# Local attention in a decoder kernel: softmax weights turned by VectorE in squares of 32, value products over 32 keys with the values stationary

## The chip, the cores and the metric

The kernel runs on one core of one Trainium2 chip. The metric is the device time of one execution in microseconds; the time before is 2144.68 us, the median of three runs (2144.33 to 2145.66). The engines of the core are TensorE (PE; the profile lists its weight loads apart, as PEld), VectorE (DVE), ScalarE (ACT), GpSimd (POOL) and SyncE (SP, which here only issues DMAs).

## The reference, cut to what matters

A decoder works on x of shape (8, 256, 128) in float32: a state-space layer, a cross attention, and then, in six layers, a local attention and a feed-forward block, each added to x. Only the local attention is touched. Per layer and batch it has 16 heads of 64 numbers and windows of 32 tokens; a window's 32 queries see its own 32 keys and the 32 of the window before:

```
q, k = l2norm(q) * q_scale, l2norm(k) * k_scale    # then rotary turns and scales
bk2, bv2 = look(bk), look(bv)                      # window before + own window: 64 keys
sim = einsum('bhwie,bhwje->bhwij', bq, bk2) * 8
sim = where(mask, -max, sim)
attn = softmax(sim, -1)
out = einsum('bhwij,bhwje->bhwie', attn, bv2)      # this product is what the change recasts
x = out.reshape(b, n, 1024) @ Wo + x
```

## The kernel before, in words

Stages 1 and 2 (state space, cross attention) fill the first 530 us or so and are not touched. Stage 3 holds the six layers. It is a pipeline over 48 "runs", one for each layer and batch. The order of the work in a run is written out by hand in the list `slots` (L1338 to L1359): four quarters, each with a query or key projection, a transposition, a piece of attention for one of four tiles, and a piece of the feed-forward block of an earlier pair of batches (`"ff"`). PE and DVE take their instructions in exactly that order (`manual_schedule`, L1482); ACT and POOL are ordered by the framework's planner; SP issues the DMAs.

Names on the way of the change, for one run n:

- `query_key` (L1041): two projections of 512 columns into PSUM (`qk_ps`, L1035), then DVE multiplies by the rotary tables (L1052, L1053), POOL adds the halves (L1056), ACT squares (`sq`, L1058), which on ACT comes after DVE's two reads of the same PSUM tile. `normalise` (L1084, POOL) and `turn` (8 transpositions on PE into `qkT_ps`, L1091, copied out by ACT) follow. `value` (L1076) projects the values of 128 tokens and ACT copies them to `v`.
- `scores` (L1126), per half `wh` of 128 tokens: 64 small products, each of 64 rows by 32 stationary columns with 64 moving ones, in eight tiles of the array (two row groups `e` by four column groups `i`). They fill the two-bank PSUM tile `s3_ps`. That tile and `o3_ps` come from `ps_two` (L72), of which there is one buffer only, so whoever fills it waits until the one before has been read out.
- Per tile t = (wh, g), g a group of eight heads: `masked` (L1147, DVE adds the mask into `pw`), `peak` (DVE maximum, POOL subtracts, L1161), `weigh` (ACT exponential), `add_weights` (DVE sum and reciprocal, POOL multiplies, L1174).
- `turn_weights` (L1176): four 128x128 transpositions on PE (L1181) and one ACT copy (L1185) put the 64 keys on the partitions.
- `place` and `spread` (L1103): per tile nine DMAs of `v` into `vz` (L1120), so that each window's 64 keys lie on 64 partitions once for each head parity; six fixed buffers are zeroed in `begin` (L1407).
- `attend` (L1188), per half: 64 products (L1198) with the weights stationary (64 rows by 32 columns) and the values moving (64 columns), in the same eight tiles. The outputs come out with queries on partitions; two DVE transpositions in squares of 32 (L1206) turn them into `oT`.
- `project_out` (L1208): eight products with `Wo` (L1212) and the addition to x. Since a square of 32 turns only inside itself, `load` (L987) brings `Wo` in eight DMAs with its rows permuted.

A matmul of float32 stands in the profile as two LDWEIGHTS and MATMUL pairs, a transposition as one; 64 products of `attend` are 128 pairs.

Of the kernel before, what the change touches and what calls it, by code (L numbers as in the profile page):

```python
# [9 lines left out]
FP = mybir.dt.float32  # L10
# [4 lines left out]
P = 128  # L15
# [35 lines left out]
def decoder_kernel(ctx: ExitStack, tc: tile.TileContext, a: dict, out: bass.AP):  # L51
# [934 lines left out]

    def load(d):  # L987
        wo = pools3["w"].tile([P, NHB, D], FP, name="wo3")

        for i in range(4):  # L990
            for g in range(2):
                f = (4 * g + i) * P
                nc.sync.dma_start(
                    out=wo[32 * i : 32 * i + 32, 4 * g : 4 * g + 4, :],
                    in_=a["L0_ffn_Wo"][d][f : f + P].rearrange("(k r) e -> r k e", r=32),
                )
        w1 = pools3["w"].tile([P, 2 * DFF], FP, name="w1")
        nc.sync.dma_start(out=w1, in_=a["L0_ffn_W1"][d])
        w2 = pools3["w"].tile([P, 3, D], FP, name="w2")
        nc.sync.dma_start(  # L1000
            out=w2[:, 0:2, :], in_=a["L0_ffn_W2"][d][0:256].rearrange("(k p) e -> p k e", p=P)
        )
        nc.sync.dma_start(out=w2[: DFF - 256, 2, :], in_=a["L0_ffn_W2"][d][256:DFF])
        wts[d] = wo, w1, w2
# [95 lines left out]
        else:  # L1100
            copied.append(A.copy(fixed3["kz"][:, :, W + tb * P : W + (tb + 1) * P], t3))  # L1101

    def spread(v, wh, g):  # L1103


        vz = fixed3["vzs"].pop(0)
        fixed3["vzs"].append(vz)
        for j in range(4):
            w = 4 * wh + j
            for e in range(2):  # L1110

                at = max(0, (w - 1) * W)
                end = (w + 1) * W
                while at < end:
                    tb = at // P
                    n = min(end, (tb + 1) * P) - at
                    k = e * HD + at - (w - 1) * W
                    src = v[tb][at - tb * P : at - tb * P + n, :]
                    src = src.rearrange("p (k e d) -> p k e d", e=2, d=HD)
                    nc.sync.dma_start(  # L1120
                        out=vz[k : k + n, j, :, :], in_=src[:, 4 * g : 4 * g + 4, e, :]
                    )
                    at += n
        return vz

    def scores(n, wh):  # L1126

# [18 lines left out]

    def masked(n, t):  # L1147
        wh, g = tiles3[t]
        shape = [P, 4, 2, 2 * W]
        pw = pools3["b"].tile(shape, FP, name="pw", bufs=5)  # L1150
        V.tensor_tensor(
            pw,
            got[n]["s_ps"][:, :, g * 256 : (g + 1) * 256].rearrange("p e (w k) -> p w e k", w=4),
            fixed3["mask"][:, 4 * wh : 4 * wh + 4, :].unsqueeze(2).to_broadcast(shape), ALU.add,
        )
        got[n]["pw", t] = pw, pools3["b"].tile([P, 2, 4, 2], FP, name="mx", bufs=5)

    def peak(n, t):
        pw, mx = got[n]["pw", t]
        V.tensor_reduce(mx[:, 0], pw, AX.X, ALU.max)  # L1160
        G.tensor_tensor(pw, pw, mx[:, 0].unsqueeze(3).to_broadcast([P, 4, 2, 2 * W]), ALU.subtract)  # L1161

    def place(n, t):
        got[n]["vz", t] = spread([got[n].get(("v", tb)) for tb in range(2)], *tiles3[t])

    def weigh(n, t):
        pw, mx = got[n]["pw", t]
# [2 lines left out]
    def add_weights(n, t):  # L1170
        pw, mx = got[n]["pw", t]
        V.tensor_reduce(mx[:, 1], pw, AX.X, ALU.add)
        V.reciprocal(mx[:, 1], mx[:, 1])
        G.tensor_tensor(pw, pw, mx[:, 1].unsqueeze(3).to_broadcast([P, 4, 2, 2 * W]), ALU.mult)  # L1174

    def turn_weights(n, t):  # L1176

        pw, mx = got[n]["pw", t]
        t_ps = ps_s("pT_ps")
        for j in range(4):  # L1180
            T.transpose(  # L1181
                t_ps[:, j * P : (j + 1) * P], pw[:, j].rearrange("p e k -> p (e k)"), ident
            )
        pT = pools3["b"].tile([P, 4, P], FP, name="pT", bufs=4)
        turned.append(A.copy(pT.rearrange("p j q -> p (j q)"), t_ps))  # L1185
        got[n]["pT", t] = pT

    def attend(n, wh):  # L1188

        o_ps = ps_two("o3_ps")  # L1190
        for g in range(2):
            pT, vz = got[n]["pT", 2 * wh + g], got[n]["vz", 2 * wh + g]
            for j in range(4):
                for i in range(4):
                    for e in range(2):
                        r = slice(e * HD, (e + 1) * HD)
                        c = (4 * g + j) * HD
                        T.matmul(  # L1198
                            o_ps[i * W : (i + 1) * W, e, c : c + HD],
                            lhsT=pT[r, j, i * W : (i + 1) * W], rhs=vz[r, j, i, :],  # L1200
                            start=True, stop=True, tile_position=(e * HD, i * W),
                        )

        oT = got[n]["oT", wh] = pools3["b"].tile([P, 2, 2, 4 * HD], FP, name="oT3")
        for g in range(2):
            V.transpose(oT[:, g], o_ps[:, :, g * 256 : (g + 1) * 256])  # L1206

    def project_out(n, wh):  # L1208
        d, b = seq[n]
        y_ps = ps_s("y3_ps")  # L1210
        for hb in range(NHB):
            T.matmul(  # L1212
                y_ps[:, :P], lhsT=wts[d][0][:, hb, :],
                rhs=got[n]["oT", wh][:, hb // 4, (hb // 2) % 2, :].rearrange(
                    "p (w h q) -> p h w q", w=4, h=2
                )[:, hb % 2],
                start=(hb == 0), stop=(hb == NHB - 1),
            )
        half = slice(wh * P, (wh + 1) * P)
        V.tensor_tensor(  # L1220
            batch(x3, b)[:, half], batch(x2 if d == 0 else x3, b)[:, half], y_ps[:, :P],
            ALU.add,
        )
        if wh:
            got[n].clear()
# [88 lines left out]
    def finish(p, b=None):  # L1314
# [22 lines left out]
    q, k = 0, 1  # L1337
    slots = [  # L1338

        (weigh, 0, 1), (place, 0, 1), (value, 1, 0), (scores, 0, 1),  # L1340
        ("end", 0), (masked, 0, 2), (masked, 0, 3), (squares, 1, k, 0), (turn, 1, q, 0),
        (peak, 0, 2), ("end", 1), ("ff",), (turn_weights, 0, 0), (add_weights, 0, 1),
        (query_key, 1, k, 1), (root, 1, k, 0), (normalise, 1, k, 0),

        ("end", 1), (weigh, 0, 2), (place, 0, 2), (project_out, -1, 0),
        (attend, -1, 1), (squares, 1, k, 1), (turn, 1, k, 0),
        (peak, 0, 3), ("end", 0), ("ff",), (turn_weights, 0, 1), (add_weights, 0, 2),
        (query_key, 2, q, 0), (root, 1, k, 1), (normalise, 1, k, 1), (shift, 3),

        (weigh, 0, 3), (place, 0, 3), (value, 1, 1), (scores, 1, 0),  # L1350
        ("end", 0), (masked, 1, 0), (masked, 1, 1), (squares, 2, q, 0), (turn, 1, q, 1),
        (peak, 1, 0), ("end", 1), ("ff",), (turn_weights, 0, 2), (add_weights, 0, 3),
        (root, 2, q, 0), ("late",), (query_key, 2, q, 1), (normalise, 2, q, 0),

        (weigh, 1, 0), (place, 1, 0), (project_out, -1, 1),
        (attend, 0, 0), (squares, 2, q, 1), (turn, 1, k, 1),
        (peak, 1, 1), ("end", 0), ("end", 1), ("ff",), (turn_weights, 0, 3), (add_weights, 1, 0),
        (query_key, 2, k, 0), (root, 2, q, 1), (normalise, 2, q, 1),
    ]  # L1359
# [36 lines left out]
    def begin():  # L1396

        for name in ("w", "a"):
            pools3[name] = ctx.enter_context(
                tc.tile_pool(name=f"s3{name}", bufs=2, side="right", reuse_waits="tile")  # L1400
            )
        fixed3["kz"] = pools3["a"].tile([P, NHB, W + S], FP, name="kz", bufs=1)
        fixed3["vzs"] = [
            pools3["a"].tile([P, 4, 4, HD], FP, name=f"vz{i}", bufs=1) for i in range(6)
        ]
        for t in [fixed3["kz"]] + fixed3["vzs"]:
            G.memset(t, 0.0)  # L1407
        fixed3["rot"] = pools3["w"].tile([P, 4, 2, HD], FP, name="rot", bufs=1)
        nc.sync.dma_start(out=fixed3["rot"], in_=a["c_rot"])
        for c in range(3):  # L1410
            load_third(0, c)
        load_table3(0)
        load(0)
        yield
        steps = [(shift, 0)]
        for c in range(2):
            for tb in range(2):
                steps += [
                    (f, 0, c, tb) for f in (query_key, squares, root, normalise)
                ]  # L1420
        for f, *args in steps:
            f(*args)
            done.add((f, *args))
            yield
# [48 lines left out]
    with ExitStack() as st:  # L1473
# [8 lines left out]
        with tc.manual_schedule(engines={mybir.EngineType.PE, mybir.EngineType.DVE}):  # L1482
            shift(1)
            for n in range(-1, len(seq)):
                run(n)
            project_out(len(seq) - 1, 0)
            attend(len(seq) - 1, 1)
            for _ in ff:
                pass
            next(end)  # L1490
            project_out(len(seq) - 1, 1)
            tail = feed_forward(DEPTH - 1, NPAIR - 1, 1)
            queue.append(finish(NPAIR - 2))
            while queue:
                next(tail, None)
                next(end)
            for _ in tail:
                pass
            for _ in finish(NPAIR - 1, 1):
                pass  # L1500
# [86 lines left out]
```

## Time and profile before

| what | value |
|---|---|
| median of three runs | 2144.68 us |
| the profiled execution | 2138.47 us |
| its span | 2136.7 us |
| granted TensorE clock, mean | 0.985 |
| stage 3, one run | about 31.3 us (two runs 62.6 us) |

The page gives the busy time of each engine, the chain of work that ended last, and groups of instructions as "line engine operation, out<-in, shapes, count | busy us, mean ns of one | idle time before them and what ended it". "Busy" of PE is no measure of load by itself, since matmuls overlap: a single matmul lasts some 216 ns here from its start to its modelled end, while the next can start a few ns later. Better is the time from the start of one group of matmuls to the start of the next, which the timeline and the chain give.

### The profile page before, as it was taken

The numbers are of one execution on the slowest core, as the hardware profiler recorded it, in microseconds if no ns is written. First come the engines' busy times: TensorE is split into PE (matmuls) and PEld (weight loads), VectorE is DVE, ScalarE is ACT, GpSimd is POOL, SyncE is SP. The second block draws the span as 40 slices with busy tenths as digits, with TensorE's granted clock in tenths as the row PEclk, the third lists the DMA queues.
The fourth block names the chain that finished last, engine by engine and source line by source line (L and its number), as shares of the span: only waits on it lengthen the run. The fifth ranks groups of instructions, "written<-read, shape, count | busy, mean of one in ns | idle before, by whom it ended". The sixth has DMA issues, their size and how long they took to land.

```text
span 2136.7 us, 77541 instructions
## 1 busy us (share of the span) xinstructions
PE 2015.2 (94%) x32582; PEld 1324.2 (62%) x32582; DVE 1728.0 (81%) x2663; ACT 1478.7 (69%) x2654; POOL 1664.9 (78%) x1466
## 2 busy tenths in 40 slices
PE   5899899899989999999999999999999999999986
PEld 3355454455566766667676666767666667676663
DVE  6778888786688888888888888888888888888752
ACT  5767867666667677777677777766777766767654
POOL 4778878887699888888888888888888887888740
PEclk8999999999999999999999999999999999999998
DMA  5433333333244343444434444443444434333330
GB/s 131 90 62 74 68 71 74 70 74 80 55 75 71 68 97 68 78 72 74 89 68 79 70 82 76 75 77 64 94 69 73 76 69 84 64 65 68 61 56 10
DMA packets 455194, 156.11 MB, mean 73 GB/s; under 512 B 402046, under 2 KB 451068, under 8 KB 454716
## 3 DMA queue, kind: packets, MB, share of 16 engines
q1 hardware_dynamic: 454364, 150.76, 37.4%
q8 instruction: 256, 4.19, 0.9%
q14 instruction: 94, 0.77, 0.1%
q10 hardware_dynamic: 480, 0.38, 0.1%
HBM read 55.33 MB, written 1.31 MB: 27 GB/s over the span
## 4 chain that ended last, share of the span: by engine, by line
PE 78%; ACT 10%; DVE 9%; issue 1%; POOL 1%; DMA 0%; ACTq 0%; POOLq 0%; DVEq 0%
PE qk_ps L1035 13%; PE y_ps L1212 8%; PE qkT_ps L1091 8%; PE o_ps L1198 7%; PE f_ps L1282 6%; PE v_ps L1035 6%; PE s_ps L1139 5%; PE pT_ps L1181 3%; PE y L645 3%; PE f_ps L1310 3%; PE o_ps L340 2%; PE s_ps L318 2%; PE k_ps L273 1%; DVE rb L1053 1%; DVE m L625 1%
## 5 line engine op out<-in xcount | busy, mean ns | idle before, releaser
L1056 POOL TENSOR_TENSOR qk<-qk,rb 128x512 f32<-128x512 f32 x384 | 481.3, 1276 | 51.2 <-DVE rb L1053 33.5
L1084 POOL TENSOR_TENSOR qk<-qk,rn 128x1024 f32<-128x1024 f32 x192 | 365.8, 1905 | 11.6 <-ACT rn L99 11.6
L1035 PE MATMUL qk_ps<-wqkv,xs 128*128 128x512 f32 x768 | 363.0, 595 | 1.6 <-ACT kz L1101 1.6
L1161 POOL TENSOR_TENSOR pw<-pw,mx 128x512 f32<-128x512 f32 x192 | 202.1, 1053 | 165.8 <-DVE mx L1160 165.6
L1058 ACT ACTIVATE sq<-qk_ps 128x1024 f32<-128x1024 f32 x192 | 197.1, 1026 | 167.6 <-PE o_ps L1198 114.9
L1052 DVE TENSOR_TENSOR qk<-qk_ps,tab 128x1024 f32<-128x1024 f32 x192 | 229.0, 1193 | 72.5 <-PE qk_ps L1035 71.0
L1053 DVE TENSOR_TENSOR rb<-qk_ps,tab 128x1024 f32<-128x1024 f32 x192 | 233.3, 1215 | 0.0
L1065 DVE TENSOR_REDUCE ss<-sq 128x16 f32<-128x1024 f32 x192 | 229.3, 1194 | 4.8 <-ACT sq L1058 4.8
L1174 POOL TENSOR_TENSOR pw<-pw,mx 128x512 f32<-128x512 f32 x192 | 200.7, 1046 | 39.5 <-ACT fxn L1269 32.0
L1212 PEld LDWEIGHTS y_ps<-oT,wo 128*128 128x128 f32 x1536 | 186.6, 192 | 46.6 <-issue 33.5
L1091 PE MATMUL qkT_ps<-ident,qk 128*128 128x128 f32 x1536 | 210.0, 279 | 3.5 <-POOL qk L1084 3.0
L607 POOL TENSOR_TENSOR dw<-wz 128x512 f32<-128x512 f32 x128 | 133.2, 1041 | 102.8 <-DVE wz L605 98.9
L1206 DVE STREAM_TRANSPOSE oT<-o_ps 128x512 f32<-128x512 f32 x192 | 126.2, 696 | 80.4 <-PE o_ps L1198 80.4
L1035 PEld LDWEIGHTS qk_ps<-wqkv,xs 128*128 128x128 f32 x768 | 131.3, 191 | 96.2 <-issue 93.2
L1212 PE MATMUL y_ps<-oT,wo 128*128 128x128 f32 x1536 | 187.7, 275 | 1.9 <-ACT pT L1185 1.6
L1139 PEld LDWEIGHTS s_ps<-kz,qT 64*32 64x32 f32 x12288 | 137.6, 105 | 76.4 <-issue 36.2
L1035 PE MATMUL v_ps<-wqkv,xs 128*128 128x512 f32 x384 | 180.8, 593 | 0.1
L1091 PEld LDWEIGHTS qkT_ps<-ident,qk 128*128 128x128 f32 x1536 | 165.2, 141 | 23.3 <-POOL qk L1084 3.8
L627 POOL TENSOR_TENSOR mc<-m,rows 128x512 f32<-128x512 f32 x128 | 163.0, 1273 | 13.3 <-PE y L645 5.2
L625 DVE TENSOR_TENSOR_SCAN m<-dw,ab 128x256 f32<-128x256 f32 x256 | 160.6, 669 | 11.9 <-ACT ab L99 8.0
L1198 PE MATMUL o_ps<-vz,pT 64*32 64x64 f32 x12288 | 167.4, 225 | 1.2 <-issue 1.2
L99 ACT ACTIVATE pw<-pw 128x512 f32<-128x512 f32 x192 | 120.7, 629 | 66.9 <-POOL pw L1161 66.9
(209 smaller groups left out, 4082.6 us busy)
## 6 DMA issues: line engine op xcount, KB each, us to landing
vz<-v SPq DMA_DIRECT2D x1152, 64.0 KB, 2.2
rows<-bc_dram SPq DMA_DIRECT2D x128, 256.0 KB, 4.7
vz<-v SPq DMA_DIRECT2D x576, 32.0 KB, 2.3
wqkv<-in_L_ffn_Wqkv SPq DMA_DIRECT2D x18, 512.0 KB, 5.0
wo<-in_L_ffn_Wo SPq DMA_DIRECT2D x48, 64.0 KB, 3.0
w<-in_L_ffn_W SPq DMA_DIRECT2D x6, 341.0 KB, 3.5
t_in<-in_x SPq DMA_DIRECT2D x4, 256.0 KB
wkv<-in_L_xattn_Wkv SPq DMA_DIRECT2D x1, 1024.0 KB
```

What stands on the lines that cost most here:

```text
L1035: T.matmul(pr[:, i * 512 : (i + 1) * 512], lhsT=got[n]["xs"][:, tb * P : (tb + 1) * P], rhs=thirds[seq[n][0], c][:, i * 512 : (i + 1) * 51 ...
L1052: V.tensor_tensor(t, p3, cs, ALU.mult)
L1053: V.tensor_tensor(rb, p3, sn, ALU.mult)
L1056: G.tensor_tensor(t[:, :, o], t[:, :, o], rb[:, :, f], ALU.add)
L1065: V.tensor_reduce(got[n]["ss"][:, 2 * c + tb, :], got[n]["sq"], AX.X, ALU.add)
L1084: G.tensor_tensor(t, t, r, ALU.mult)
L1091: T.transpose(t_ps[:, hb * P : (hb + 1) * P], t[:, 2 * hb : 2 * hb + 2, :].rearrange("p h d -> p (h d)"), ident,)
L1139: T.matmul(s_ps[i * W : (i + 1) * W, e, c : c + 2 * W], lhsT=qT[r, 4 * g + i, j * W : (j + 1) * W], rhs=kz[r, 4 * g + i, k0 : k0 + 2 * W], ...
L1161: G.tensor_tensor(pw, pw, mx[:, 0].unsqueeze(3).to_broadcast([P, 4, 2, 2 * W]), ALU.subtract)
L1174: G.tensor_tensor(pw, pw, mx[:, 1].unsqueeze(3).to_broadcast([P, 4, 2, 2 * W]), ALU.mult)
L1198: T.matmul(o_ps[i * W : (i + 1) * W, e, c : c + HD], lhsT=pT[r, j, i * W : (i + 1) * W], rhs=vz[r, j, i, :], start=True, stop=True, tile_p ...
L1212: T.matmul(y_ps[:, :P], lhsT=wts[d][0][:, hb, :], rhs=got[n]["oT", wh][:, hb // 4, (hb // 2) % 2, :].rearrange("p (w h q) -> p h w q", w=4 ...
```

## The change

`turn_weights` becomes one DVE transposition in squares of 32, from SBUF to SBUF. Inside each square 32 queries by 32 keys change places, so that the keys of a window lie on 32 partitions `i` (a pair of heads) and their two query windows (own and next) lie side by side. `attend` takes the values as the stationary operand (32 rows of keys by 64 columns of one head) and the weights as the moving one (64 columns, or 32 at the edge of a half), and adds up in PSUM over the windows. It is called twice for each half (`part`), each time with two of the four row groups, because each row group writes to its own bank. The outputs come out turned, so an ACT copy takes the place of the DVE transpositions. `pw` changes the order of its axes; `place` fills one `vz` tile per 128 tokens by 16 DMAs; `Wo` is loaded in one DMA; the zeroing goes.

```diff
     def load(d):
-        for i in range(4):
-            for g in range(2):
-                f = (4 * g + i) * P
-                nc.sync.dma_start(out=wo[32 * i : 32 * i + 32, 4 * g : 4 * g + 4, :], ...)
+        nc.sync.dma_start(out=wo, in_=a["L0_ffn_Wo"][d].rearrange("(k p) e -> p k e", p=P))
...
+    def place(n, tb):
+        vz = got[n]["vz", tb] = pools3["a"].tile([P, 4, 2, P], FP, name="vz", bufs=6)
+        src = got[n]["v", tb].rearrange("p (g i c) -> p g i c", g=2, i=4)
+        for w in range(4):
+            for i in range(4):
+                nc.sync.dma_start(
+                    out=vz[i * W : (i + 1) * W, w], in_=src[w * W : (w + 1) * W, :, i, :]
+                )
...
     def turn_weights(n, t):
         pw, mx = got[n]["pw", t]
-        t_ps = ps_s("pT_ps")
-        for j in range(4):
-            T.transpose(
-                t_ps[:, j * P : (j + 1) * P], pw[:, j].rearrange("p e k -> p (e k)"), ident
-            )
-        pT = pools3["b"].tile([P, 4, P], FP, name="pT", bufs=4)
-        turned.append(A.copy(pT.rearrange("p j q -> p (j q)"), t_ps))
+        pT = got[n]["pT", t] = pools3["b"].tile([P, 2, 2 * P], FP, name="pT", bufs=4)
+        V.transpose(
+            pT.rearrange("p e c -> p (e c)"), pw.rearrange("p e w k -> p (e w k)")
+        )
-    def attend(n, wh):
-        o_ps = ps_two("o3_ps")
-        for g in range(2):
-            for j in range(4):
-                for i in range(4):
-                    for e in range(2):
-                        r = slice(e * HD, (e + 1) * HD)
-                        c = (4 * g + j) * HD
-                        T.matmul(
-                            o_ps[i * W : (i + 1) * W, e, c : c + HD],
-                            lhsT=pT[r, j, i * W : (i + 1) * W], rhs=vz[r, j, i, :],
-                            start=True, stop=True, tile_position=(e * HD, i * W),
-                        )
-        oT = got[n]["oT", wh] = pools3["b"].tile([P, 2, 2, 4 * HD], FP, name="oT3")
-        for g in range(2):
-            V.transpose(oT[:, g], o_ps[:, :, g * 256 : (g + 1) * 256])
+    def attend(n, wh, part):
+        o_ps, first = ps_two("o3_ps"), True
+        for js in ((0, 2), (-1, 1, 3) if wh else (1, 3)):
+            for g, j in ((g, j) for g in range(2) for j in js):
+                pT, w = got[n]["pT", 2 * wh + g], 4 * wh + j
+                vz = got[n]["vz", w // 4]
+                lo, hi = max(j, 0) * W, min(j + 2, 4) * W
+                at = max(2 * j + 1, 0) * W
+                for b in range(2):
+                    i = 2 * part + b
+                    r = slice(i * W, (i + 1) * W)
+                    c = g * P
+                    for e in range(2):
+                        T.matmul(
+                            o_ps[e * HD : (e + 1) * HD, b, c + lo : c + hi],
+                            lhsT=vz[r, w % 4, g, e * HD : (e + 1) * HD],
+                            rhs=pT[r, e, at : at + hi - lo],
+                            start=first, stop=bool(g and j == 3), tile_position=(i * W, e * HD),
+                        )
+                first = False
+        if not part:
+            got[n]["oT", wh] = pools3["b"].tile([P, 2, 2, 2 * P], FP, name="oT3")
+        turned.append(A.copy(got[n]["oT", wh][:, part], o_ps[:, :, : 2 * P]))
...
     slots: second quarter
-        ("end", 1), (weigh, 0, 2), (place, 0, 2), (project_out, -1, 0),
-        (attend, -1, 1), (squares, 1, k, 1), (turn, 1, k, 0),
+        ("end", 1), (weigh, 0, 2), (place, 1, 0), (attend, -1, 1, 0), (project_out, -1, 0),
+        (squares, 1, k, 1), (turn, 1, k, 0), (attend, -1, 1, 1),
     slots: fourth quarter
-        (weigh, 1, 0), (place, 1, 0), (project_out, -1, 1),
-        (attend, 0, 0), (squares, 2, q, 1), (turn, 1, k, 1),
+        (weigh, 1, 0), (place, 1, 1), (attend, 0, 0, 0), (project_out, -1, 1),
+        (squares, 2, q, 1), (turn, 1, k, 1), (attend, 0, 0, 1),
...
-        for t in [fixed3["kz"]] + fixed3["vzs"]:
-            G.memset(t, 0.0)
+        G.memset(fixed3["kz"], 0.0)
```

The two other `place` calls of the first and third quarter go, and after the last run `attend(…, 1, 0)`, `project_out(…, 0)` and `attend(…, 1, 1)` follow each other in that order.

## The prediction

> **What bounds the kernel now.** I read the page first (busy shares, then the chain that ended last), then the windows over two runs of stage 3, the chain inside one stretch, and the timeline around one `attend`.
>
> ```profile
> PE 2015.2 (94%) x32582; PEld 1324.2 (62%) x32582; DVE 1728.0 (81%) x2663; ACT 1478.7 (69%) x2654; POOL 1664.9 (78%) x1466
> ...
> PE 78%; ACT 10%; DVE 9%; issue 1%; POOL 1%; DMA 0%; ACTq 0%; POOLq 0%; DVEq 0%
> ```
>
> ```profile
> 1187.90:1250.50 62.60, 61.92 (x1274) 43.58 (x1264) 53.75 (x77) 44.65 (x79) 51.39 (x45) 1.00 0.39 68
> ```
>
> The second fence is two runs of stage 3: PE busy 61.92 of 62.60 us, weight loads 43.58, DVE 53.75, ACT 44.65, POOL 51.39, clock 1.00. PE has no holes to fill; the others have 9 to 18 us of air. So in stage 3 a nanosecond of PE's stream is a nanosecond of the time, in 48 runs, until another engine runs out of air. The chain in one stretch gives PE's price list (start, us, what):
>
> ```profile
> 1397.40 0.44 PE pT_ps L1181 x4
> 1397.84 1.72 PE qk_ps L1035 x4
> 1399.56 1.78 PE y_ps L1212 x16
> 1401.34 1.70 PE o_ps L1198 x107
> 1403.04 1.02 PE qkT_ps L1091 x8
> ```
>
> **The sums on PE, each against the profiled execution (2138.47 us, span 2136.7; it lies 6.2 us under the median of the runs shown, and I subtract the result from the median).**
>
> Removed: 768 transpositions (L1181), four in 0.44 us: 192 x 0.437 = 84 us.
>
> Removed and added: `attend`. The old burst takes 1.70 us from its start to the next group's, plus a switch in front of it:
>
> ```profile
> 1400.86 1.22 DVE L1053 TENSOR_TENSOR rb<-qk_ps,tab 128x1024 f32<-128x1024 f32 x1
> 1401.07 0.28 PE L1212 MATMUL y_ps<-oT,wo 128*128 128x128 f32 x1
> 1401.27 1.61 PEld L1198 LDWEIGHTS o_ps<-vz,pT 64*32 64x32 f32 x128
> 1401.27 1.77 PE L1198 MATMUL o_ps<-vz,pT 64*32 64x64 f32 x128
> 1401.99 0.28 DVE L1220 TENSOR_TENSOR y<-y,y_ps 128x128 f32<-128x128 f32 x1
> 1402.17 1.02 ACT L1058 ACTIVATE sq<-qk_ps 128x1024 f32<-128x1024 f32 x1 [2.67 <-PE o_ps L1198]
> ...
> 1402.97 0.86 PEld L1091 LDWEIGHTS qkT_ps<-ident,qk 128*128 128x128 f32 x8
> 1402.97 1.09 PE L1091 MATMUL qkT_ps<-ident,qk 128*128 128x128 f32 x8
> 1403.13 1.31 DVE L1206 STREAM_TRANSPOSE oT<-o_ps 128x512 f32<-128x512 f32 x2 [0.87 <-PE o_ps L1198]
> ```
>
> The last `y_ps` starts at 1401.07 and o_ps at 1401.27: 0.20 us, where `y_ps` matmuls follow each other in 1.78/16 = 0.11. So going into tiles costs 0.09. On the way out the last o_ps starts about 0.15 before 1402.97, of which 0.054 is its own streaming (below), so 0.09 again. Old half: 0.09 + 1.70 = 1.79 us.
>
> The new rate is not in the trace and has to be built. 512 columns take 1.72/4 = 0.43 us, so a column costs 0.84 ns and 64 columns 54 ns. The first 32 matmuls of an old burst stand in its first 0.26 us (windows 1401.27 to 1401.53): eight tiles run side by side, four rounds of about 55 ns and one load. [...] Bounds: 8.1 ns if it ran like the first 0.26 us, 27 ns if only two tiles overlapped, as in stage 2:
>
> ```profile
> L340 PEld LDWEIGHTS o_ps<-w,v x512: 132/137/137, 108.0 to 569.4; 128*64 128x64 f32 x171
> L340 PE MATMUL o_ps<-w,v x512: 379/379/431, 108.0 to 569.6; 128*64 128x256 f32 x171
> ```
>
> These are the nearest rows for 64 stationary columns (minimum, median, maximum ns): a load lasts 137 ns against 106 for 32 columns (L1198) and 190 for 128 (L1035), some 0.8 ns a column, and a matmul that has to wait for its load lasts 431 instead of 379, 52 ns more. So a load of 64 columns takes about 52 ns and is just covered by the 54 ns of the matmul before it in the same tile. A matmul of 32 columns (27 ns) doesn't cover it, so I let these cost a full round. I take 55 ns a round, the row of four concurrent tiles being nearest to the eight of the same kind of burst.
>
> A part of the first half has 8 (g, j) of 8 pairs: 64 pairs, 16 rounds. In the second half the window before the half comes in too: 10, so 80 pairs, 20 rounds. Each burst: 0.09 in, 0.05 first load, rounds, 0.10 out: 16 x 0.055 + 0.24 = 1.12, and 20 x 0.055 + 0.24 = 1.34; with the stagger of the last round 1.14 and 1.36. A half has two bursts: 2.28 or 2.72, mean 2.50. Against 1.79 that is +0.71 us, in 96 halves +68 us. Half of this is the second switch and load (0.24), the rest the longer rounds.
>
> PE: -84 + 68 = -16 us.
>
> [...]
>
> **What lies beside PE.** DVE: 192 transpositions of 128x512 go (1.31 us for two, 80.4 us of waiting for o_ps in front of them) and 192 come, from SBUF. Their price: L1172, reading 512 from SBUF, takes 676 ns, L1151 from PSUM 685; so 0.66 to 0.70 us, equal to before. They move: one in each quarter, so the first and third quarter get 0.69 more (they have 6.4 to 7.7 of 7.6 to 10.0 us now) and the others 0.65 less and no wait. Behind each stands only `add_weights`; the product it waits for (L1174) ended 4 us earlier (1401.70 against about 1406). Cover gone: 0.1 to 0.7 us in a quarter. There is a gain too: PE waits 14.0 us in all (22 times) at L1282 for `sq`, which comes behind DVE's rotary reads, and the second quarter in front of it gets some 1 us earlier on DVE. I count -8, bounds 0 and -14.
>
> ACT: a copy of 0.59 us goes from each quarter (L1185) and two come in the second and fourth: equal in sum. But now the PSUM pair `two` is freed by ACT three times in half a run where DVE did it twice. Behind `part` 1 waiting on PE stand the feed-forward piece, the next projection, all of PE. Its cover is `project_out` and `turn`: 1.78 + 1.02 = 2.8 us. In the quarter with the Gelu (two table loads of 1.28 and 1.83 of work, in 23 of 96 halves) ACT is full until 3.5 us after the quarter's start, and the copy comes out 0.3 late or more: I count +8, bounds 0 and +30.
>
> DMA: 1728 issues of `vz` become 1536, by 0.63 us each on SP, about 92 MB become 50, in pieces of twice the length. The values are placed about one run before they are read (16 issues are 10 us, landing 2.2). Bounds 0 and -2: ACT's 19 us of waiting for these reads ended before PE needed the copy. `Wo` in one DMA, and the six memsets (5.4 us of POOL) that end at 521.6, when POOL waits 8.3 us for a transfer anyway: 0. The end of the last run gets one burst more: within 1.
>
> Sum: -16 - 8 + 8 = -16 us: 2144.7 - 16 = 2129. With the bounds of the edits that are hidden, and 8 us of either sign for the switch and the rounds, 2105 to 2145.
>
> **The rivals.**
>
> *The second burst waits for ACT (slower).* Place: ACT's queue in quarters two and four. In the timeline `sq` sits idle there for 2.67 us until DVE ends L1053 at 1402.08, and ends itself at 1403.19. The planner decides whether the copy of part 0 stands before or behind it. Before: ready at about 1399.4 + 1.14, hidden. Behind: done at 1403.8, and PE, which would start part 1 at 1399.4 + 1.14 + 1.78 + 0.93 = 1403.25, waits 0.55 us, plus up to 0.7 where DVE is late from the quarter before. From 0.17 us a half it eats the 16 us. At 0.3 to 1.1 us, mean 0.6: 96 x 0.6 = +58, so 2187. For it: ACT is strictly in order. Against: elsewhere ACT takes what is ready first (the exponential at 1398.86 stands ahead of the older `sq`).
>
> *Edges are cheap (faster still).* If loads are hidden better, matmuls of 32 columns cost half a round: 4 and 8 of them in rounds per part, 24 a run, x 27 ns x 48 = -31: 2098.
>
> *DVE becomes the bound (no change).* In quarters one and three DVE would have about 7.5 us of work, PE 7.3. If nothing evens this out, 0.2 x 96 = 19 us come back: 2148.
>
> *Row groups of 32 overlap only by twos (the change costs more than it removes).* No row shows four tiles of 32 rows. Then 27 ns a pair: 144 x 27 + 0.48 = 4.4 us a half, +2.6 x 96 = 250, less 84: 2311.
>
> **How the numbers follow.** Forecast 0.53, ACT's wait 0.21, cheap edges 0.12, DVE 0.08, twos 0.06. 0.2% (4.3 us) is about what a measurement of this kernel can tell from no change. Faster by more: 0.43 of the forecast's 0.53 and the cheap edges, 0.55. Within: 0.08 from the forecast, 0.04 from DVE, 0.12. Slower: the rest, 0.33. The range reaches from the cheap edges with their bound (2092) to ACT's wait (2188); outside lie the twos and the upper half of ACT's wait. The likeliest case by itself: 2105 to 2145.
>
> **What would show it.** PE still at 98 to 99% in stage 3; L1181 gone; o_ps in two bursts a half, 0.9 and 1.1 us from first start to last, with 13 to 14 ns from start to start; 13824 MATMUL records of o_ps; ACT's copies of o_ps ahead of `sq`; a run about 0.3 us shorter. Wrong if a gap of half a microsecond stands in front of the second burst, or the bursts last 2 us.

## The result, and the profile after

The changed kernel takes **2194.21 us** (median of four runs, 2191.41 to 2197.59) against 2144.51 us for the kernel before (four runs, 2140.53 to 2145.66): a ratio of 1.0236, with a 95% interval from 1.0213 to 1.0259, so some 50 us slower. The prediction had said 16 us faster, with a range of 2092 to 2188. The profiled execution took 2196.7 us, its span is 2194.9.

From its page, the busy time, the packets of the DMA, and the chain that ended last:

```profile
PE 2024.2 (92%) x33350; PEld 1302.2 (59%) x33350; DVE 1720.7 (78%) x2663; ACT 1484.2 (68%) x2654; POOL 1661.2 (76%) x1460
...
DMA packets 181105, 112.03 MB, mean 51 GB/s; under 512 B 29662, under 2 KB 176988, under 8 KB 180636
...
PE 58%; DVE 22%; ACT 14%; POOL 3%; issue 2%; DMA 1%; SPq 0%; ACTq 0%; POOLq 0%; DVEq 0%
```

DVE and ACT, 9 and 10% of the chain before, are now 22 and 14%: PE waits for another engine. One window over two runs of stage 3 (span of the window, then PE, weight loads, DVE, ACT, POOL busy, granted clock, DMA share, GB/s) says how long:

```profile
1234.08:1298.99 64.91, 61.84 (x1296) 42.50 (x1295) 53.54 (x77) 45.00 (x78) 51.64 (x45) 1.00 0.18 43
```

Two runs took 62.60 us, of which PE worked 61.92. They take 64.91, and PE works 61.84. So PE has hardly less to do than before, where 0.7 us less was forecast, and it now stands idle for 3.07 us instead of 0.68. Those are two separate errors. The idle time has a list of its own; these are PE's waits between 700 and 1950 us (what waited, what it waited for, us in all, times, the longest):

```profile
PE f_ps L1261 <- ACT sq L1051: 37.2, 19, 2.0
PE qkT_ps L1084 <- ACT v L1071: 17.4, 19, 0.9
PE o_ps L1176 <- ACT oT L1185: 2.5, 13, 0.2
```

Before, the first of these was 12.8 us, 20 times. All 19 stand in one of the eight quarters of two runs, the one after the feed-forward's normalisation (the bad quarter, below). There the timeline of PE, of ACT and of DVE reads (start, duration, what, and in brackets the idle time before it and what ended it):

```profile
1404.67 1.13 PE L1245 MATMUL ln_var<-ln_sq,mean_w 128*128 128x512 f32 x2
...
1411.55 1.09 PE L1084 MATMUL qkT_ps<-ident,qk 128*128 128x128 f32 x8 [0.91 <-ACT v L1071]
1414.60 2.84 PE L1261 MATMUL f_ps<-fxn,w 128*128 128x512 f32 x6 [1.96 <-ACT sq L1051]
```

```profile
1406.16 0.22 ACT L99 ACTIVATE rn<-rn 128x16 f32<-128x16 f32 x1
1406.29 0.57 ACT L1185 COPY oT<-o_ps 128x512 f32<-128x512 f32 x1
1407.19 0.63 ACT L99 ACTIVATE pw<-pw 128x512 f32<-128x512 f32 x1 [0.34 <-POOL pw L1141]
1407.73 0.67 ACT L99 ACTIVATE ln_sq<-ln_var,eps_t 128x512 f32<-128x512 f32 x1
1408.43 0.63 ACT L99 ACTIVATE ln_sq<-ln_sq 128x512 f32<-128x512 f32 x1
```

```profile
1409.09 0.75 DVE L1247 SCALAR_TENSOR_TENSOR fxn<-ln_xc,cols,ln_sq 128x512 f32<-128x512 f32 x1 [3.05 <-ACT ln_sq L99]
1409.77 0.70 DVE L1157 STREAM_TRANSPOSE pT<-pw 128x512 f32<-128x512 f32 x1
1410.39 0.64 DVE L1149 TENSOR_REDUCE mx<-pw 128x8 f32<-128x512 f32 x1
...
1412.28 1.22 DVE L1046 TENSOR_TENSOR rb<-qk_ps,tab 128x1024 f32<-128x1024 f32 x1
```

The variance product `ln_var` starts at 1404.67 and the next group on PE at 1405.63, so ACT could take its logarithm soon after. But in ACT's queue, which the planner orders, Ln and Exp on `ln_sq` now stand behind the root of the keys' norm (`ss`, `rn`), the copy of the second burst (`oT`) and an exponential (`pw`) that waits for POOL. Ln starts at 1407.73. DVE stands still for 3.05 us at `fxn`, and behind `fxn` in its fixed order are the turning of the weights, `add_weights` and the rotary reads. Those end at 1413.5, ACT's `sq` comes at 1413.53, and PE waits 1.96 us. The same stretch of the kernel before, ACT and DVE:

```profile
1370.99 1.01 ACT L1101 COPY kz<-qkT_ps 128x1024 f32<-128x1024 f32 x1 [0.47 <-PE qkT_ps L1091]
1371.90 0.69 ACT L99 ACTIVATE ln_sq<-ln_var,eps_t 128x512 f32<-128x512 f32 x1
1372.48 0.59 ACT L1185 COPY pT<-pT_ps 128x512 f32<-128x512 f32 x1
1372.95 0.65 ACT L99 ACTIVATE ln_sq<-ln_sq 128x512 f32<-128x512 f32 x1
```

```profile
1373.63 1.14 DVE L1268 SCALAR_TENSOR_TENSOR fxn<-ln_xc,cols,ln_sq 128x512 f32<-128x512 f32 x1 [0.53 <-ACT ln_sq L99]
```

Ln stood directly behind the copy of the keys, and DVE waited 0.53 us.

**The ledger of two runs** (us), worked out from the traces over twenty double runs (a double run is two runs). Each group of PE counts from its first start to the first start of the next group, less PE's idle time, which has its own row. The last three columns are kernels of the experiments below (runs 1, 2 and 4). A dash means that the kernel has no such work.

| | before | after | ACT's order | burst moved | burst and turning moved |
|---|---|---|---|---|---|
| PE's transpositions of the weights | 3.50 | - | - | - | - |
| `o_ps` (attend) | 6.72 | 9.44 | 9.44 | 9.44 | 9.44 |
| `s_ps` (scores, code unchanged) | 6.19 | 5.72 | 5.65 | 5.65 | 5.66 |
| all other groups | 45.49 | 47.21 | 46.64 | 46.59 | 46.55 |
| PE idle | 0.71 | 3.05 | 1.33 | 0.80 | 0.00 |
| two runs | 62.61 | 65.43 | 63.06 | 62.49 | 61.67 |

### The profile page after: what moved, and what is told of

It reads as the page before. It is cut to its first block, busy times and chain, and to the rows that moved or that the text cites. A ratio compares the mean times of both kernels' runs of the same rounds, so it can differ in the third digit from the quotient of the medians.

```text
span 2194.9 us, 77233 instructions
## 1 busy us (share of the span) xinstructions
PE 2024.2 (92%) x33350; PEld 1302.2 (59%) x33350; DVE 1720.7 (78%) x2663; ACT 1484.2 (68%) x2654; POOL 1661.2 (76%) x1460
## 2 busy tenths in 40 slices
DMA packets 181105, 112.03 MB, mean 51 GB/s; under 512 B 29662, under 2 KB 176988, under 8 KB 180636
## 4 chain that ended last, share of the span: by engine, by line
PE 58%; DVE 22%; ACT 14%; POOL 3%; issue 2%; DMA 1%; SPq 0%; ACTq 0%; POOLq 0%; DVEq 0%
PE qk_ps L1028 10%; PE o_ps L1176 6%; PE v_ps L1028 5%; PE f_ps L1261 5%; PE s_ps L1119 4%; PE y_ps L1191 4%; PE qkT_ps L1084 4%; DVE ss L1058 3%; PE y L645 3%; DVE rb L1046 3%; PE f_ps L1289 3%; DVE qk L1045 3%; ACT sq L1051 3%; PE o_ps L340 2%; DVE pw L1131 2%; PE s_ps L318 2%
## 5 line engine op out<-in xcount | busy, mean ns | idle before, releaser
L1176 PEld LDWEIGHTS o_ps<-pT,vz 32*64 32x64 f32 x13824 | 218.9, 133 | 94.3 <-issue 64.9
L1176 PE MATMUL o_ps<-pT,vz 32*64 32x64 f32 (+1 forms) x13824 | 240.5, 218 | 4.7 <-ACT oT L1185 2.5
L1028 PEld LDWEIGHTS qk_ps<-wqkv,xs 128*128 128x128 f32 x768 | 146.3, 192 | 155.6 <-issue 128.2
L1084 PE MATMUL qkT_ps<-ident,qk 128*128 128x128 f32 x1536 | 205.4, 277 | 23.9 <-ACT v L1071 20.2
L1261 PE MATMUL f_ps<-fxn,w 128*128 128x512 f32 (+3 forms) x288 | 153.0, 658 | 52.0 <-ACT sq L1051 43.0
L1191 PE MATMUL y_ps<-oT,wo 128*128 128x128 f32 x1536 | 197.0, 281 | 0.1
L1084 PEld LDWEIGHTS qkT_ps<-ident,qk 128*128 128x128 f32 x1536 | 170.3, 142 | 36.8 <-ACT v L1071 23.3
L1191 PEld LDWEIGHTS y_ps<-oT,wo 128*128 128x128 f32 x1536 | 178.7, 191 | 4.5 <-DVE y L1290 0.5
L1119 PEld LDWEIGHTS s_ps<-kz,qT 64*32 64x32 f32 x12288 | 127.5, 105 | 72.9 <-issue 32.6
```

The lines of the kernel that those rows point to most:

```text
L1028: T.matmul(pr[:, i * 512 : (i + 1) * 512], lhsT=got[n]["xs"][:, tb * P : (tb + 1) * P], rhs=thirds[seq[n][0], c][:, i * 512 : (i + 1) * 51 ...
L1084: T.transpose(t_ps[:, hb * P : (hb + 1) * P], t[:, 2 * hb : 2 * hb + 2, :].rearrange("p h d -> p (h d)"), ident,)
L1119: T.matmul(s_ps[i * W : (i + 1) * W, e, c : c + 2 * W], lhsT=qT[r, 4 * g + i, j * W : (j + 1) * W], rhs=kz[r, 4 * g + i, k0 : k0 + 2 * W], ...
L1176: T.matmul(o_ps[e * HD : (e + 1) * HD, b, c + lo : c + hi], lhsT=vz[r, w % 4, g, e * HD : (e + 1) * HD], rhs=pT[r, e, at : at + hi - lo], ...
L1191: T.matmul(y_ps[:, :P], lhsT=wts[d][0][:, hb, :], rhs=got[n]["oT", wh].rearrange("p a b (g q) -> p g a b q", g=2)[:, hb // 4, (hb // 2) % ...
L1261: T.matmul(o, lhsT=w1[:, i * DFF + f0 : i * DFF + f0 + n], rhs=xn, start=True, stop=True)
```

## The experiments

Theory A: the planner's new order in ACT's queue is the cause. Rivals: the second burst stands ahead of the feed-forward's product on PE and delays its chain by itself (B), or DVE's turning of the weights, now ahead of `add_weights` and the rotary reads, does it (C). Besides these, three things are tested: the premise "PE's stream is the time", the price of a burst (the time that one burst of small products takes beyond its products), and the faster scores.

**1. ACT takes Ln and Exp first** (`act_first`).

```diff
-        inv_root(sq, var, eps_t)
+        normed.append(inv_root(sq, var, eps_t))          # in feed_forward
...
-        with tc.issue_after(copied[-1].ins) if copied else ExitStack():
+        with (tc.issue_after(copied[-1].ins) if copied else ExitStack(),
+              tc.issue_after(normed[-1].ins) if normed else ExitStack()):
             with_table(A.activation, ss, ss, AF.Relu, bias=tiny[:, 0:1])   # root
...
+        with tc.issue_after(normed[-1].ins) if normed else ExitStack():
             with_table(A.activation, pw, pw, AF.Exp)     # weigh
```

> The changed kernel with one thing different: ACT's queue takes the feed-forward's Ln and Exp on ln_sq ahead of the root's and the weights' work, in every quarter. PE's and DVE's orders stay as they are. Theory A (in one quarter of eight the planner put Ln and Exp behind root, copy and exponential, so DVE stands 3.05 us at fxn, is late with the rotary reads, and PE waits for sq and v and loses clock in the gaps): DVE's wait at fxn falls from 3.05 to about 0.5 us in that quarter, PE's gaps from 3.05 to about 1 us per two runs, and the half-clock windows go: 24 x (2.3 + 0.5) = 67 us, so 2125 to 2140. Theory B (the second burst stands ahead of the feed-forward's matmul on PE, and ACT's order is only where that shows): ln_var comes as late as before this edit, 24 x at most 0.7 us of wait is saved, 2175 to 2195. Theory C (DVE's turning of the weights stands ahead of add_weights and the rotary reads): no change, 2185 to 2200.

Measured: 2143.71 us, ratio to the kernel before 1.0014 (1.0001 to 1.0027). With PE's and DVE's orders untouched, 50 us are gone. DVE's wait at `fxn` is down to 1.23 us, not to the 0.5 expected, which is why the time lies a little above the band of theory A; PE's wait for `sq` is 1.12. The two waits between 700 and 1950 us, and ACT in that quarter:

```profile
DVE fxn L1251 <- ACT ln_sq L99: 23.4, 19, 1.2
PE f_ps L1265 <- ACT sq L1051: 21.3, 19, 1.1
...
1444.47 0.69 ACT L99 ACTIVATE ln_sq<-ln_var,eps_t 128x512 f32<-128x512 f32 x1 [0.30 <-PE ln_var L1249]
1445.19 0.63 ACT L99 ACTIVATE ln_sq<-ln_sq 128x512 f32<-128x512 f32 x1
```

Ln now waits for PE, no longer for ACT's own queue. Theory A holds for the main part; B keeps a smaller one: `ln_var` itself still comes a burst later than before (runs 4 and 5 say what the place of the burst is worth).

**2. The second burst behind the feed-forward piece** (`late_burst`).

```diff
-        (squares, 1, k, 1), (turn, 1, k, 0), (attend, -1, 1, 1),
-        (peak, 0, 3), ("end", 0), ("ff",), (turn_weights, 0, 1), ...
+        (squares, 1, k, 1), (turn, 1, k, 0),
+        (peak, 0, 3), ("end", 0), ("ff",), (attend, -1, 1, 1), (turn_weights, 0, 1), ...
```

and the same in the fourth quarter.

> The changed kernel with one thing different: the second burst of a half stands behind the feed-forward piece on PE instead of ahead of it. Theory A: it helps only because the planner then puts Ln and Exp early on ACT too (it does in the order that was built), so it comes out like the run that changes ACT's queue alone, 2125 to 2145. Theory B: it is the part that matters, and is faster than the run that changes ACT's queue alone by 30 us or more. Theory C: no change, 2185 to 2200.

Measured: 2134.99 us, ratio 0.9976 (0.9965 to 0.9987), below the kernel before. It is 9 us better than run 1, far from the 30 that theory B asked for. Moving the burst also gave the planner an order with Ln early, so this run alone could not have told A from B. PE's only wait in stage 3 is again the one of before:

```profile
PE f_ps L1261 <- ACT sq L1051: 16.0, 20, 0.8
```

**3. DVE turns the weights behind the rotary reads** (`dve_late`).

```diff
-        ("ff",), (turn_weights, 0, 0), (add_weights, 0, 1),
-        (query_key, 1, k, 1), (root, 1, k, 0), ...
+        ("ff",), (add_weights, 0, 1),
+        (query_key, 1, k, 1), (turn_weights, 0, 0), (root, 1, k, 0), ...
```

in each quarter.

> The changed kernel with one thing different: DVE's turning of the weights stands behind the projection's rotary reads in each quarter, not ahead of add_weights. Theory A and theory B: Ln and Exp stay late on ACT; DVE reads the projection 0.70 us sooner in every quarter, so the wait of PE for sq shrinks by at most that: 24 x 0.7 = 17 us in the bad quarter, 2172 to 2200. Theory C: the 0.70 us of each quarter were what made PE wait, the PE gaps fall back to 0.7 us per two runs and the time to about 2135.

Measured: 2188.59 us, ratio 1.0228 (1.0205 to 1.0251): 6 us less than the change by the medians, 2 by the ratios, whose intervals overlap. Theory C falls: moving the turning doesn't bring the time back. PE's waits between 700 and 1950 us show where the 0.70 us went:

```profile
PE f_ps L1261 <- ACT sq L1051: 25.9, 19, 1.4
PE qkT_ps L1084 <- ACT v L1071: 21.9, 19, 1.2
PE o_ps L1176 <- ACT oT L1185: 14.1, 18, 0.8
```

The wait for `sq` fell from 37.2 to 25.9 us, and the second burst's wait for ACT's copy of part 0 rose from 2.5 to 14.1, the wait for `v` from 17.4 to 21.9.

**4. The burst and the turning both moved** (`late_dve`, edits 2 and 3, which are those of runs 2 and 3).

> The run with the second burst behind the feed-forward piece, and besides that DVE's turning of the weights behind the projection's rotary reads in each quarter. ACT's queue stays the same. Left in that run is one stall of PE per two runs, about 0.96 us, where the feed-forward's first product waits for sq. If the 0.70 us of the turning in DVE's queue make it, it shrinks to 0.3 and the time by 24 x 0.7 = 17 us, 2115 to 2122. If the wait comes from the chain of the normalisation alone, no change, 2131 to 2140; slower than that if the turned weights or add_weights are now late for the burst.

Measured: **2112.94 us**, ratio 0.9876 (0.9851 to 0.9901), faster than both kernels. Two runs of it:

```profile
1428.25:1489.92 61.67, 61.67 (x1295) 42.09 (x1294) 54.70 (x77) 44.60 (x78) 51.54 (x45) 1.00 0.17 37
```

PE has no idle time left: 61.67 of 61.67. So with ACT's order good and the second burst moved, the 0.70 us of DVE's turning are the last wait, 0.80 us per two runs, and moving them is worth 22 us. In run 3 the same edit was worth 6 at most; run 5 asks which of the two made the difference.

**5. Both queues mended, PE's order as in the change** (`act_dve`, edits 1 and 3).

> The changed kernel with its order on PE as it is, and both other edits: ACT takes the feed-forward's Ln and Exp first, and DVE turns the weights behind the projection's rotary reads. If the two waits are separate and PE's order does no harm of its own, the gains add where both had room: 2143.7 less the 17 to 22 us that the second edit gave behind a good ACT queue, 2120 to 2127. If the second burst's place on PE costs by itself (PE waited 0.19 us per two runs for ACT's copy of part 0, and the product of the feed-forward starts a burst later), it stays some 10 us above the run with both the burst and the turning moved, 2120 and more; if the two edits fight for the same 0.7 us, 2135 to 2145.

Measured: 2138.21 us, ratio 0.9986 (0.9975 to 0.9997). The gains do not add. PE's waits between 700 and 1950 us:

```profile
PE o_ps L1180 <- ACT oT L1189: 15.6, 20, 0.8
PE f_ps L1265 <- ACT sq L1051: 10.0, 19, 0.5
```

In run 1 the wait for `sq` was 1.1 us a time and the second burst's wait for ACT's copy of part 0 was 0.2; here they are 0.5 and 0.8. What one gave, the other took, as in run 3. This second wait is the one that the prediction feared (a copy of part 0 late in the quarter with the Gelu); in the changed kernel it costs 2.5 us in these 1250. So moving DVE's turning is worth at most 6 us with ACT's order bad (run 3) and 5.5 with it mended (this run against run 1), as long as the second burst stands ahead of the feed-forward piece; with the burst moved it is worth 22. The place of the burst makes the difference here, 25 us between this run and run 4, where PE never waits for that copy. Theory B had the wrong size for the change as it was built, and a part of the truth for a kernel whose other waits are gone.

**6. What is a removed transposition worth?** Two runs with the kernel before. In `b_no_turn` ACT copies the weights unturned:

```diff
-        for j in range(4):
-            T.transpose(t_ps[:, j * P : (j + 1) * P], ...)
-        turned.append(A.copy(pT.rearrange("p j q -> p (j q)"), t_ps))
+        turned.append(A.copy(pT.rearrange("p j q -> p (j q)"), pw.rearrange("p w e k -> p (w e k)")))
```

> The kernel before without the four PE transpositions of a tile of weights: ACT copies the weights unturned from SBUF, so the turning of the weights is left out and nothing stands in for it. This asks what the removal alone is worth. If PE sets the period in stage 3, as the prediction had it, the whole 192 x 0.437 = 84 us come back: 2055 to 2070. If the removed work only uncovers waits for DVE and ACT (DVE's 53.75 and POOL's 51.39 of 62.60 us per two runs, in chains that then end last), half or less comes back: 2100 to 2145.

Measured: 2271.52 us, ratio 1.0613 (1.0594 to 1.0633): 130 us slower with 768 instructions of PE taken out. Neither expectation had that. ACT's longest waits between 700 and 1950 us:

```profile
ACT pT L1180 <- POOL pw L1174: 266.3, 127, 3.5
```

The copy now depends on POOL's product directly, and ACT stands up to 3.5 us in front of it with everything else queued behind; PE's idle time per two runs goes from 0.7 to 7.6 us. The run says nothing of PE's share, and much of ACT's order. So the second, `b_one_turn`, keeps one transposition of four, and ACT copies the one turned window four times over; PE stays between POOL and ACT:

```diff
-        for j in range(4):
+        for j in range(1):
...
-        turned.append(A.copy(pT.rearrange("p j q -> p (j q)"), t_ps))
+        turned.append(A.copy(pT, t_ps[:, :P].unsqueeze(1).to_broadcast([P, 4, P])))
```

> The kernel before with one PE transposition of a tile of weights instead of four; ACT copies the one turned window four times over, so three windows of four are left without their own turning. ACT still waits for PE at the same places, and its queue is as before but for the copy of the weights, which stands two places sooner in a few quarters. If PE sets the period in stage 3 (a ns of PE's stream is a ns of the time), 192 x 3 x 0.109 = 63 us go: 2072 to 2090. If the freed time turns into waits for ACT and DVE, half of it or less goes: 2110 to 2145.

Measured: 2094.42 us, ratio 0.9785 (0.9764 to 0.9806): 47 of the 63 us, between the two expectations. In the trace PE's transpositions shrink by 2.62 us per two runs and the period by 2.10; the wait for `sq` grows from 0.64 to 0.96 a time, and small losses in other groups take the rest. So PE's stream is most of the time, and most of what is lost goes to the one place where a chain beside PE is nearly as long.

**7. Both parts in one burst** (`one_burst`, and `one_dve` with edit 3 besides).

```diff
-        o_ps, first = ps_two("o3_ps"), True
+        o_ps, first = ps_big("o3_ps") if part else ps_two("o3_ps"), True
+        if part:
+            o_ps = o_ps.rearrange("p (b c) -> p b c", b=2)
...
-        ... (attend, -1, 1, 0), (project_out, -1, 0),
-        (squares, 1, k, 1), (turn, 1, k, 0), (attend, -1, 1, 1),
+        ... (attend, -1, 1, 0), (attend, -1, 1, 1), (project_out, -1, 0),
+        (squares, 1, k, 1), (turn, 1, k, 0),
```

> The changed kernel with both parts of a half in one burst on PE: part 0 into its pair of banks as now, part 1 right behind it into one of the big PSUM tiles. The same products. Theory F (each burst of small tiles has a fixed price in PE's stream, read from the traces as 0.09 at its entry, 0.09 from its last start to the next group beyond its own streaming, and 0.10 more in the first pair behind it, together 0.29 us, where the prediction had 0.18 and a first load): 96 x 0.29 = 28 us less than the run with the second burst behind the feed-forward piece, 2100 to 2115, as long as ACT takes both copies in time. Rival (the price is of the pairs alone, or what PE saves turns into the wait for sq at the feed-forward's product): 2125 to 2140.

> The run with one burst a half, and besides that DVE's turning of the weights behind the projection's rotary reads. In the run with one burst PE's stream was shorter, but the transposition of the keys waited 0.4 to 0.9 us behind project_out for ACT's sq, which reads the PSUM tile that the rotation hands to it, and the gates waited 1.2. Theory G (those waits hang on sq, and sq on DVE's rotary reads): sq comes 0.7 us sooner, most of the waits go, and the price of a merged pair of bursts shows: 0.23 us in the bursts, 0.09 at one entry and 0.10 behind one exit, 0.42 a half, 96 x 0.42 = 40 us below the 2113 of the run with two bursts, less what is left of the waits (24 x 0.3 to 0.8): 2080 to 2095. Rival (the extra PSUM tile makes PE wait for sq whatever DVE does): 2110 to 2140.

Measured: `one_burst` 2156.18 us, ratio 1.0078 (1.0053 to 1.0103); `one_dve` 2127.04 us, ratio 0.9934 (0.9913 to 0.9954). The price of a burst shows where it was read: from the burst's first start to the next group 160 pairs take 2.37 us where two bursts of 80 took 2 x 1.30; the entry in the group ahead of the second burst (0.09) and the exit behind it (0.10) are gone too, 0.42 us a half. But the time did not follow: `one_burst` lies above both expectations, `one_dve` in the rival's, 14 us above `late_dve`. The extra tile from the pool of big PSUM tiles puts the transposition behind a tile that ACT still reads:

```profile
1418.69 2.05 PE L1193 MATMUL y_ps<-oT,wo 128*128 128x128 f32 x16
1421.01 1.06 PE L1084 MATMUL qkT_ps<-ident,qk 128*128 128x128 f32 x8 [0.27 <-issue]
```

```profile
1419.89 1.03 ACT L1051 ACTIVATE sq<-qk_ps 128x1024 f32<-128x1024 f32 x1 [1.54 <-DVE rb L1046]
```

16 products of `y_ps` need 1.89 us elsewhere, here the next group starts 2.32 after them, 0.09 us after `sq` ended at 1420.92. The page calls the gap "issue"; the end of `sq` is what it coincides with. With edit 3 that wait shrinks to 0.4 us and stays in one quarter (8.0 us between 700 and 1950), and the wait for `sq` at the feed-forward's product ("the gates" in the expectation) from 1.2 to 0.6. A few gaps of up to 1.6 us in `o_ps` and `y_ps`, put down to "issue" (7.8 and 8.3 us in the two runs), stay unexplained.

**8. More traffic** (`more_dma`: edit 2, and at each `place`, three DMAs of the mask into a tile that nobody reads).

```diff
+        more = pools3["b"].tile([P, 8, 80], FP, name="more", bufs=1)
+        for _ in range(3):
+            nc.sync.dma_start(out=more[:, :, : 2 * W], in_=fixed3["mask"])
```

> The run with the second burst behind the feed-forward piece, and besides that three DMAs more at each placing of the values: the mask, 1024 pieces of 256 bytes each, into a tile that nobody reads, some 295000 packets and 75 MB in all, so that the traffic is again that of the kernel before (455194 packets, 156 MB). Nothing of the computation changes. Theory D (the scores' burst, whose code was not changed, got faster because the transfers of the values no longer get in the way of PE's instructions): the scores' burst goes from 1.41 us back to 1.52 to 1.55, four times in two runs, +13 us, 2145 to 2152. Theory E (it got faster for another reason, its place behind other work): it stays at 1.41 and the time within 8 us of that run, 2130 to 2143. The planner puts ACT's second copy of o_ps a little later in some quarters here, which by itself may cost up to 8 us in either case: the length of the burst decides.

Measured: 2475.22 us, ratio 1.1565 (1.1539 to 1.1591). The time is far outside both expectations and no measure of the scores, since the added transfers stand ahead of others in SP's queue. PE waits for those:

```profile
PE o_ps L1179 <- DMA vz<-v: 65.7, 67, 3.4
PE qk_ps L1028 <- DMA wqkv<-in_L_ffn_Wqkv: 60.9, 4, 16.9
PE v_ps L1028 <- DMA wqkv<-in_L_ffn_Wqkv: 53.2, 4, 13.7
```

The length of the scores' burst does decide, as the expectation says: from the first start to the next group it is 1.53 us (median) in the kernel before, 1.41 in `late_burst` and 1.52 here, with the same code; from first to last start 1.38, 1.27 and 1.38. So the traffic lengthens it. By which way, whether through PE's instructions as theory D has it, no run shows.

## Why the prediction was wrong, step by step

Two terms failed. ACT's +8, which should have held the whole price of ACT's queue, was 40 to 50 us too small: the order of that queue changed at the feed-forward's normalisation, where the prediction did not look. And PE's sum of -16 was +2 to +8, because a burst costs more than was counted. Terms that the prediction did not have, the faster scores above all, gave some of it back.

- **"What bounds the kernel: in stage 3 a ns of PE's stream is a ns of the time, until another engine runs out of air."** Three quarters right (47 of 63 us in `b_one_turn`). The air of DVE and ACT was read as a sum over two runs (53.75 and 44.65 of 62.60), but what counts is the one chain of the eight quarters in which PE already waited, `fxn` to `sq` to the feed-forward's product.
- **"-84 us"** for the transpositions: right, 3.50 us per two runs, 24 times.
- **"Each burst 1.14 or 1.36, +0.71 us a half, +68 us": the mis-sized term.** The rounds were right (0.92 and 1.15 us from first to last start, 58 ns a round against 55, and 13824 records). (The remark that half of the 0.71 is the second switch and load is wrong by its own figures: 0.24 of 0.71 is a third.) The way out was not. The step "0.09 again" counted the time from the last start to the next group less its own streaming. Behind it the next group's first pair is slow as well: there in `late_burst` the first two starts of `y_ps` lie 0.213 us apart instead of 0.112, those of `qk_ps` 0.533 instead of 0.429 (in the kernel before, behind the old burst, those of a transposition 0.165 instead of 0.109, which could have been read). A burst is 1.25 or 1.49 (0.09 + 1.06 or 1.30 + 0.10), and with the old half at 1.84, not 1.79, attend costs 0.90 us more a half; by the ledger it is (2.72 + 1.10) / 4 = 0.95. 96 times that is +86 to +92. **PE's sum was +2 to +8, not -16.** The rows here put about 0.09 us on the way in and 0.09 plus 0.10 on the way out.
- **The scores: no step had them.** -0.54 us per two runs, -13 us, with 112 MB in 181105 packets instead of 156 in 455194 (run 8). The prediction bounded the DMA's effect by 0 and -2. With them and the longer wait for `sq` (+2) the sum is -9 to -3, and `late_burst`, whose ACT queue is in order, measured 0.9976, 5 us less than the kernel before.
- **"DVE: equal price"**: right per instruction (0.70 us). **"The wait for `sq` shrinks, -8"**: wrong in sign. Even with ACT's order mended by moving the burst it was 0.80 us instead of 0.64, since the turning stands ahead of the rotary reads; moving it away as well gave 22 us (run 4). "Behind each stands only `add_weights`" was the failing sentence: behind `add_weights` stand the reads that PE waits for a quarter later.
- **"ACT: equal in sum, the Gelu quarter +8"**: the step that failed most. Where the prediction looked it was about right: the copy of part 0 stands ahead of `sq` in three of the four halves of two runs and behind it in the one with the Gelu (`sq` at 1421.74, the copy at 1422.64), and there PE waited 0.2 us a time, 2.5 us between 700 and 1950 us. But moving work on PE and DVE had the planner order ACT anew, and one of the eight quarters got Ln and Exp behind a copy and an exponential. Run 1, which changes ACT's queue alone, takes 50 us of this back. Against `late_burst`, where the burst is moved besides, it is 59 us between the two medians and 2.94 us per two runs: 2.25 as idle PE, 0.62 in "all other groups", most of it at a lower clock (PE's work is 62.38 in the ledger and 61.84 in the two runs above, where the clock was 1.00). With these 59 the sum above becomes +50 to +56; measured is +50.
- **The rivals.** "The second burst waits for ACT" gave 2187, the nearest time, by the wrong wait, so its nearness is chance. Its kind is right (ACT's order, set by the planner) and its place is not: it was not the copy of part 0 but the normalisation. Its own wait is real and shows with 0.8 us a time once DVE's turning is moved, with Ln late (run 3) as with Ln early (run 5). DVE as the bound: no, DVE has 7 us of air per two runs when PE has none (run 4). Cheap edges: no, the rounds with 32 columns cost full ones in sum, as assumed (two such rounds start 30 ns apart, but the step back to 64 columns then takes 86 instead of 58). Overlap by twos: no, four pairs start in 58 ns.
- **"What would show it"** did its work: "PE still at 98 to 99% in stage 3" is 95% (61.84 of 64.91), and a double run got 2.3 us longer instead of 0.6 shorter. The named sign of failure, a gap of half a microsecond ahead of the second burst, did not come: the longest was 0.2.

What stays open: why the planner chose that order. That moving the burst changes it is shown; which of its costs or due times tipped it is not.

## What to carry to other kernels

Where a planner orders a queue, moving any operation may reorder all of them: read the new queue's order around the one chain that PE already waits for, before counting gains on another engine. Count for each burst of small tiles the way in, the way out, and the slow first pair behind it (0.09, 0.09 and 0.10 us here), and ask whether the change makes more bursts. What an edit is worth depends on which wait ends last: the same 0.70 us on DVE were worth 6 us at most where the second burst then waited for ACT's copy, whether ACT's order was bad or mended, and 22 where the burst stood elsewhere.

## What the runs showed of the hardware

- **The clock was halved after some of the bad quarters.** In the kernel before, the granted clock stays at 1.00 between 700 and 1950 us. In the changed kernel the clock is 0.50 in seven windows of 3.41 us, which follow seven of the nineteen bad quarters, in which PE is idle for 0.9 us and, after 1.1 us of work, for 2.0. The same two stretches in a quarter where it drops:

```profile
1215.00:1218.40 3.40, 1.09 (x8) 0.86 (x8) 3.40 (x5) 2.08 (x5) 2.02 (x2) 0.96 0.13 29
1218.40:1221.80 3.40, 3.35 (x5) 1.45 (x6) 3.25 (x6) 2.92 (x6) 2.97 (x4) 0.54 0.25 55
```

  The eighth figure is the clock: 0.54 in the 3.4 us behind the gap. In run 1, where PE is idle for 1.1 us in these quarters, and in run 2, with 0.8, it was 1.00 from 700 to 1900 us.

  The seven drops of the changed kernel last 3.413 us each in the clock's record and start whole multiples of that apart (64.85 us is 19 of them, 327.68 is 96). Cut at these multiples, the stretch just ahead of each drop has 1.95 to 1.96 us of PE idle time (four cases) or 2.32 (three). The stretches of the other twelve quarters have 1.79 to 1.94 (eleven cases) and 1.96 (one), so the idle time doesn't tell all of them apart. In `one_burst` (run 7) the clock falls to 0.50 at 1353.32 and 1735.61 us, though PE is busy by the profile for 2.85 and 2.75 of the 3.41 us ahead. Most of both stretches is a burst of 160 pairs, and one gap follows it, of 0.73 and 1.16 us. Why the clock falls there, no run shows.
- **The scores' burst, with a pair in about 10 ns, was longer under more DMA traffic**: its 128 pairs took 1.38 us from first to last start (median) at a DMA share of about 0.4 and 1.27 at 0.2. The new bursts of `attend`, at 14.5 ns a pair, had the same median length (0.916 and 1.149 us) in `late_burst` and under the traffic of `more_dma`.
- **Two bursts joined were shorter than two apart** even inside: in `one_burst` 160 pairs took 2.22 us from first to last start, two bursts of 80 took 2 x 1.15.
